# Perceiver block on one core: first norm of the prologue split between VectorE and ScalarE, root table and value weights moved in ScalarE's load list

## Chip, core and metric

The kernel runs on one core of a Trainium2 chip. The metric is device time in microseconds of one execution; the median of three runs is compared. Engines are called as the profile calls them: PE (TensorE), DVE (VectorE), ACT (ScalarE), POOL (GpSimd) and SP (SyncE). ACTq and SPq are the instruction queues of ScalarE and SyncE, from which loads are issued.

## What is computed

Two sequences of 512 tokens with 512 features pass through three stages, each added to its input:

```python
x = x + xattn(layernorm(x), ctx, mask, Wq, Wk, Wv, Wo)   # 16 heads; 8192 context rows of 384
x = x + attn(layernorm(x), ...)                          # causal, amplitude and phase, 16 heads
x = x + moe(layernorm(x), ...)                           # 16 experts, two per token, capacity 64
layernorm: (x - mean) / sqrt(var + 1e-5)                 # over the 512 features
```

All is float32. The mask of the cross-attention is given as bytes; masked keys get a large negative bias. Only the first layernorm, ahead of the cross-attention, is touched by the change (a helper that a later stage calls too is rewritten for both).

## The kernel before

Tokens lie in eight tiles of 128 (four for each sequence, `TB` = 4). The cross-attention runs over 16 chunks of 1024 context rows (eight for each sequence) and, within each, over four groups of four heads; all of its matmuls are on TensorE, in four column or row strips at a time (`columns`, L216). It takes most of the span.

Ahead of that loop stands a prologue, `prepare` (L290 to L402). From L569 on, instructions keep the written order on each engine, so what a line comes behind in the text is what it comes behind on its queue. The prologue does the following:

- Loads. SyncE issues four token tiles of sequence 0 (L294), the mask and the context of chunk 0 in six loads of 256 KB (L256, L260), the tokens of sequence 1 (L304, 1 MB), the mask and context of chunk 1 (three loads of 512 KB) and Wo (L306). ScalarE issues the mask as a table (L296), four slices of Wq (L299), three of Wk and three of Wv (L302).
- The first key that isn't masked is found for each sequence (L309 to L345), and its context column is gathered by six indirect loads of POOL (L354), three for each sequence, with an index from VectorE for each (L353).
- The norm of sequence 0: `pieces[0]` to `pieces[3]` are the statistics of a tile (`stats`, L101), with the search for the first key between them; `pieces[4]` is `scale` (L106), which takes the root of all four variances on ScalarE (L82), its reciprocal and one Newton step on VectorE (L83 to L87); `pieces[5]` to `pieces[8]` scale a tile on VectorE (`normed`, L110 to L121).
- Each tile is turned by four TensorE transposes into PSUM (L193) and copied out by ScalarE (L194). When all four are turned, `query(0, 0)` projects the queries of the first head group (32 matmuls, L373), and `first_keys(0)` projects the gathered key (L376 to L389).

After that come the keys of the first step (L420), the maxima of the scores, and a list of further work beside them (`beside`, L589): the norm of sequence 1, the other queries, the values (which read Wv for the first time) and `first_keys(1)`.

`scale_of`, `scaled` and `normed` are also offered to a later stage (L895 to L911), which calls them with a tile to keep (`keep`): three tiles' root, scaling on ScalarE, then the fourth.

```python
def scaled(i):
    if i == 0:
        nc.vector.scalar_tensor_tensor(less[:, :TB-1], mv[:, :TB-1, 0], -1.0, rstd[:, :TB-1], ...)
    tiles.append(keep[:, i, :])
    nc.scalar.activation(tiles[-1], xs[...], AF.Identity, bias=less[:, i:i+1], scale=rstd[:, i:i+1])
```

Of the kernel before, what the change touches and what calls it, by code (L numbers as in the profile page):

```python
# [11 lines left out]
F32 = mybir.dt.float32  # L12
# [3 lines left out]
AF = mybir.ActivationFunctionType  # L16
# [4 lines left out]
P = 128  # L21
B, S, D = 2, 512, 512
H, HD = 16, 32
NT = B * S // P
TB = S // P
ND = D // P
M, CD = 8192, 384
NC = CD // P
# [14 lines left out]
def perceiver_kernel(ctx: ExitStack, tc: tile.TileContext, a, out: bass.AP):  # L43
    nc = tc.nc
# [26 lines left out]
    def m4(name, shape=(P, 2, S)):  # L71
        return mid.tile(list(shape), F32, tag="m4", name=name)
# [5 lines left out]
    def inv_sqrt(pool, y, v, tag):  # L78

        shape = list(v.shape)  # L80
        t = pool.tile(shape, F32, tag=f"{tag}_t", name=f"{tag}_t")
        nc.scalar.activation(t, v, AF.Sqrt)  # L82
        nc.vector.reciprocal(y, t)  # L83
        nc.vector.tensor_tensor(t, y, y, ALU.mult)
        nc.vector.tensor_tensor(t, t, v, ALU.mult)
        nc.vector.tensor_scalar(t, t, -0.5, 1.5, ALU.mult, ALU.add)
        nc.vector.tensor_tensor(y, y, t, ALU.mult)  # L87

    lnp = ctx.enter_context(tc.tile_pool(name="ln", bufs=2))
    eps = const.tile([P, 1], F32, name="eps")  # L90
    nc.gpsimd.memset(eps, LN_EPS)

    def norm_pieces(b, keep=None, aside=False):


        pool = lnp
        mv = pool.tile([P, TB, 2], F32, tag="ln_mv", name="ln_mv")
        v = pool.tile([P, TB], F32, tag="ln_v", name="ln_v")
        rstd = pool.tile([P, TB], F32, tag="ln_r", name="ln_r")

        def stats(i):  # L101
            st = pool.tile([P, 6], F32, tag="ln_st", name="ln_st")
            nc.vector.bn_stats(st, xs[:, b * TB + i, :])
            nc.vector.bn_aggr(mv[:, i, :], st)

        def scale():  # L106
            nc.vector.tensor_scalar_add(v, mv[:, :, 1], LN_EPS)
            inv_sqrt(pool, rstd, v, "ln")

        def normed(i):  # L110
            if keep is not None:
                xn = keep[:, i, :]
            elif i % 2 == 0:
                tiles.pair = m4("ln_xn", (P, 2, D))
                xn = tiles.pair[:, 0, :]
            else:
                xn = tiles.pair[:, 1, :]
            nc.vector.tensor_scalar(
                xn, xs[:, b * TB + i, :], mv[:, i, 0:1], rstd[:, i : i + 1], ALU.subtract, ALU.mult
            )  # L120
            tiles.append(xn)  # L121

        less = pool.tile([P, TB], F32, tag="ln_less", name="ln_less")
        t = pool.tile([P, TB], F32, tag="ln_t2", name="ln_t2")

        def newton():
            nc.vector.reciprocal(rstd, t)
            for out, x, y in ((t, rstd, rstd), (t, t, v)):
                nc.gpsimd.tensor_tensor(out, x, y, ALU.mult)
            nc.gpsimd.tensor_scalar(t, t, -0.5, 1.5, ALU.mult, ALU.add)  # L130
            nc.gpsimd.tensor_tensor(rstd, rstd, t, ALU.mult)
            nc.gpsimd.tensor_tensor(less, mv[:, :, 0], rstd, ALU.mult)
            nc.gpsimd.tensor_scalar(less, less, -1.0, None, ALU.mult)

        def normed_aside(i):
            if i % 2 == 0:
                tiles.pair = m4("ln_xn", (P, 2, D))
            tiles.append(tiles.pair[:, i % 2, :])
            nc.scalar.activation(
                tiles[-1], xs[:, b * TB + i, :], AF.Identity, bias=less[:, i : i + 1], scale=rstd[:, i : i + 1]  # L140
            )

        class Tiles(list):
            pass

        tiles = Tiles()

        def scale_of(lo, hi):

            some = slice(lo, hi)  # L150
            nc.scalar.activation(t[:, some], mv[:, some, 1], AF.Sqrt, bias=eps)
            nc.vector.tensor_scalar_add(v[:, some], mv[:, some, 1], LN_EPS)
            nc.vector.reciprocal(rstd[:, some], t[:, some])
            nc.vector.tensor_tensor(t[:, some], rstd[:, some], v[:, some], ALU.mult)
            nc.vector.tensor_tensor(t[:, some], t[:, some], rstd[:, some], ALU.mult)
            nc.vector.tensor_scalar(t[:, some], t[:, some], -0.5, 1.5, ALU.mult, ALU.add)
            nc.vector.tensor_tensor(rstd[:, some], rstd[:, some], t[:, some], ALU.mult)

        def scaled(i):

            if i == 0:
                nc.vector.scalar_tensor_tensor(
                    less[:, : TB - 1], mv[:, : TB - 1, 0], -1.0, rstd[:, : TB - 1], ALU.mult, ALU.mult
                )
            tiles.append(keep[:, i, :])
            nc.scalar.activation(
                tiles[-1], xs[:, b * TB + i, :], AF.Identity, bias=less[:, i : i + 1], scale=rstd[:, i : i + 1]
            )

        tiles.stats, tiles.scale_of, tiles.scaled, tiles.normed = stats, scale_of, scaled, normed  # L170
        pieces = [lambda i=i: stats(i) for i in range(TB)]
        if aside:
            pieces += [
                lambda: nc.gpsimd.tensor_scalar(v, mv[:, :, 1], LN_EPS, None, ALU.add),
                lambda: nc.scalar.activation(t, v, AF.Sqrt),
                newton,
            ]
        else:
            pieces += [scale]
        pieces += [lambda i=i: (normed_aside if aside else normed)(i) for i in range(TB)]  # L180
        return tiles, pieces
# [48 lines left out]
    def cross_attention(tail):  # L230

        with ExitStack() as st:
# [17 lines left out]
            def load_chunk(i, pieces=1):  # L250
                b, c = chunks[i]
                t = [m4("ctx", (P, CH)) for j in range(NC)]
                src = a["ctxT"][b].rearrange("(c p) k -> p c k", p=P)
                m8 = sm.tile([P, CH], U8, tag="m8", name="m8")
                row = a["mask_BxS2_bf1"][b : b + 1, c * CH : (c + 1) * CH]
                nc.sync.dma_start(m8, row.to_broadcast([P, CH]))  # L256
                for hf in range(pieces):
                    at = slice(hf * CH // pieces, (hf + 1) * CH // pieces)
                    for j in range(NC):
                        nc.sync.dma_start(t[j][:, at], src[:, j, c * CH + at.start : c * CH + at.stop])  # L260
                ctx_tiles[i], mask_tiles[i] = t, m8

            wkv = [m4("wkv", (P, 2, D)) for _ in range(NC)]
            wk, wv = ([wkv[j // 2][:, j % 2, :] for j in range(n, n + NC)] for n in (0, NC))
# [25 lines left out]
            def prepare(qp):  # L290
# [6 lines left out]
                wq = b8("wq")  # L297
                for c in range(ND):
                    nc.scalar.dma_start(wq[:, c, :], a["L0_xattn_Wq"][c * P : (c + 1) * P, :])  # L299
                for w, n in ((wk, "Wk"), (wv, "Wv")):  # L300
                    for j in range(NC):
                        nc.scalar.dma_start(w[j], a[f"L0_xattn_{n}"][j * P : (j + 1) * P, :])  # L302
                load_chunk(0, 2)
                nc.sync.dma_start(xs[:, TB:, :], x_in[:, TB:, :])  # L304
                load_chunk(1)
# [18 lines left out]
                tiles, pieces = norm_pieces(0)  # L324
# [22 lines left out]
                cf1 = [qp.tile([P, 1], F32, name=f"cf_{i}") for i in range(NC * B)]  # L347
                cf = qp.tile([P, NC, B], F32, name="cf")
                table = a["ctxT"].rearrange("b c (k o) -> (b c k) o", o=1)
                for b in range(B):  # L350
                    for c in range(NC):
                        i = c * B + b
                        nc.vector.tensor_scalar(at_i[i], at[:, b : b + 1], float((b * CD + c * P) * M), None, ALU.add)  # L353
                        nc.gpsimd.indirect_dma_start(  # L354
                            out=cf1[i],
                            out_offset=None,
                            in_=table,
                            in_offset=bass.IndirectOffsetOnAxis(ap=at_i[i], axis=0),
                        )
                anyb = qp.tile([P, B], F32, name="anyb")  # L360
                nc.vector.tensor_scalar_min(anyb, pf[:, :B], 1.0)
                nc.vector.tensor_scalar(kmul, anyb, is_bias, BIG, ALU.mult, ALU.mult)
# [4 lines left out]
                def turned(b, tiles, i):  # L367
                    turn(Bank(bank()), "j", tiles[i], xnT[b][:, :, i * P : (i + 1) * P], nc.scalar.copy)
# [19 lines left out]
                            )  # L388
                    nc.vector.tensor_copy(kf[:, :, b], pk[:, :NG])  # L389

                for f in pieces[3:5]:
                    f()
                for i in range(TB):
                    pieces[5 + i]()
                    turned(0, tiles, i)
                query(0, 0)
                first_keys(0)
                tiles, pieces = norm_pieces(1)
# [170 lines left out]
            ctx.enter_context(tc.manual_schedule())  # L569
            with tc.tile_pool(name="xa_q", bufs=1) as qp:  # L570
                norm, more = prepare(qp)

                def keys_of(n, hf):
# [48 lines left out]
            for n, (i, g) in enumerate(steps):  # L622
                b, c = chunks[i]
                pieces = [(k_half, n + 2, hf) for hf in range(2)] if n + 2 < len(steps) else [None] * 2
# [11 lines left out]
                for kt in range(NKT):  # L636
# [17 lines left out]
                    else:  # L654
                        part = None
                        if pieces[kt // 2]:
                            f, k, x = pieces[kt // 2]
# [924 lines left out]
```

## Time and profile before

| what | value |
| --- | --- |
| median of three runs | 2997.42 us (2994.43 to 2998.41) |
| time of the profiled execution | 2998.28 us |
| its span, first to last instruction | 2996.6 us |
| mean granted clock of TensorE | 0.987 |
| TensorE busy from 0 to 30 us | 16.35 us |
| TensorE busy from 60 to 2350 us | 2285.87 us |
| mean DMA share and rate from 0 to 30 us | 0.89, 308 GB/s |

The profile lists for each engine what ran, from when and for how long, and for idle time the event that ended it. The chain of work is followed back from the last instruction to what released it. A wait is put down to the releaser that came last. Durations of DMA issues are those of the issuing instruction; from the first of a group to the end of its last, waits between are counted in.

### The profile page before, as it was taken

What the parts mean: (1) busy time and instruction counts of PE and PEld (TensorE: products, weight loads), DVE (VectorE), ACT (ScalarE), POOL (GpSimd) and SP (SyncE); (2) the same over time, 40 slices, a digit from 0 to 9 for tenths busy, and PEclk for the clock granted to TensorE, in tenths of its full rate; (3) what the DMA queues carried; (4) which work ended last, traced back from release to release, by engine and by line L of the source; (5) the groups of instructions that cost most, each with busy time, mean ns of one, the idle gap of its engine ahead of it and who ended that gap; (6) DMA issues with size and microseconds to landing.
All of it is one profiled execution on the core that took longest, in us unless ns stands there. A gap on an engine that the chain in (4) does not pass through costs nothing.

```text
span 2996.6 us, 65645 instructions
## 1 busy us (share of the span) xinstructions
PE 2912.9 (97%) x28459; PEld 1128.1 (38%) x28459; DVE 1960.1 (65%) x3292; ACT 1397.1 (47%) x2614; POOL 2177.5 (73%) x880
## 2 busy tenths in 40 slices
PE   7999999999999999999999999999999999999985
PEld 2333333333333333333333333333333332345574
DVE  5567776677777677766777777777767666556422
ACT  1345555555555555544555555555555436563311
POOL 1598888888888888978888888888888872012022
PEclk9999999999999999999999999999999999999988
DMA  3000000000000000000000000000000002001374
GB/s 124 1 24 2 24 2 24 1 24 2 24 3 23 5 21 9 17 1 24 2 24 1 24 1 24 1 24 1 24 2 1 29 29 72 1 29 62 103 249 138
DMA packets 48145, 89.73 MB, mean 30 GB/s; under 512 B 4720, under 2 KB 23152, under 8 KB 47856
## 3 DMA queue, kind: packets, MB, share of 16 engines
q1 hardware_dynamic: 40832, 70.31, 7.0%
q0 software_dynamic: 2752, 8.39, 0.9%
q10 hardware_dynamic: 4272, 6.83, 0.7%
q8 instruction: 223, 3.65, 0.5%
q14 instruction: 66, 0.54, 0.1%
HBM read 77.13 MB, written 8.39 MB: 29 GB/s over the span
## 4 chain that ended last, share of the span: by engine, by line
PE 93%; DVE 3%; ACT 1%; DMA 1%; issue 1%; POOL 0%; ACTq 0%; POOLq 0%; DVEq 0%
PE s L220 31%; PE s L449 18%; PE s L514 16%; PE s L462 15%; PE s L481 4%; PE s L1244 2%; PE ph L953 2%; PE s L541 2%; PE po L970 1%; DVE cm L471 1%; PE s L1338 1%; PE s L1379 1%; DVE acc L549 1%; DMA r<-results,get 0%; DVE acc L529 0%
## 5 line engine op out<-in xcount | busy, mean ns | idle before, releaser
L680 POOL TENSOR_TENSOR es<-es,e 128x2048 f32<-128x2048 f32 x374 | 1700.7, 4547 | 54.9 <-ACT e L483 38.1
L483 ACT ACTIVATE e<-s 128x512 f32<-128x512 f32 x2048 | 1057.4, 603 | 1111.0 <-PE s L481 1111.0
L471 DVE TENSOR_REDUCE cm<-s 128x1 f32<-128x512 f32 x2048 | 1271.0, 683 | 332.3 <-PE s L449 332.2
L449 PE MATMUL s<-k,qT 32*128 32x512 f32 x4096 | 588.1, 641 | 3.4 <-DVE cm L471 1.9
L462 PE MATMUL s<-qT,k 32*128 32x512 f32 x4096 | 554.8, 593 | 3.1 <-ACT e L483 2.3
L514 PE MATMUL s<-e,v 128*32 128x512 f32 x4096 | 495.3, 600 | 1.1 <-DVE cm L471 1.0
L680 POOL TENSOR_TENSOR es<-e 128x2048 f32<-128x2048 f32 x63 | 286.1, 4541 | 242.9 <-ACT e L483 242.9
L220 PE MATMUL s<-wkv,ctx 128*32 128x512 f32 x3072 | 365.4, 596 | 0.4
L220 PE MATMUL s<-ctx,wkv 128*32 128x512 f32 x3072 | 356.5, 597 | 0.5
L462 PEld LDWEIGHTS s<-qT,k 32*128 32x128 f32 x4096 | 282.3, 184 | 185.1 <-issue 106.3
L529 DVE TENSOR_TENSOR acc<-acc,s 128x512 f32<-128x512 f32 (+1 forms) x359 | 207.8, 604 | 138.6 <-PE s L514 138.1
L449 PEld LDWEIGHTS s<-k,qT 32*128 32x128 f32 x4096 | 161.8, 183 | 330.7 <-issue 259.0
L514 PEld LDWEIGHTS s<-e,v 128*32 128x32 f32 x4096 | 107.4, 109 | 320.0 <-DVE cm L471 160.9
L481 PE MATMUL s<-rows,mb 4*128 4x512 bf16 x2048 | 218.0, 376 | 0.0
L425 DVE SCALAR_TENSOR_TENSOR k<-s,kf,m 128x512 f32<-128x512 f32 x128 | 96.1, 751 | 171.7 <-PE s L220 171.7
L220 PEld LDWEIGHTS s<-ctx,wkv 128*32 128x32 f32 x3072 | 87.2, 109 | 236.5 <-issue 155.5
L220 PEld LDWEIGHTS s<-wkv,ctx 128*32 128x32 f32 x3072 | 86.9, 109 | 214.3 <-issue 125.9
L440 ACT COPY v<-s 128x512 f32<-128x512 f32 x128 | 74.9, 585 | 98.7 <-PE s L220 77.8
L537 DVE TENSOR_TENSOR acc<-acc,s 128x1024 f32<-128x1024 f32 x56 | 68.4, 1221 | 71.1 <-ACT s L536 71.1
L1325 POOL TENSOR_SCALAR_AFFINE_SELECT e<-e 128x512 f32<-128x512 f32 x32 | 22.3, 708 | 120.0 <-ACT e L1323 120.0
L481 PEld LDWEIGHTS <-mb 4*128 4x128 bf16 x2048 | 68.5, 93 | 105.5 <-issue 97.4
L1293 POOL TENSOR_TENSOR rest<-scm,parts 128x16 f32<-128x16 f32 x8 | 2.0, 253 | 124.3 <-DVE parts L1291 121.2
(277 smaller groups left out, 1917.0 us busy)
## 6 DMA issues: line engine op xcount, KB each, us to landing
ctx<-in_ctxT_dram SPq DMA_DIRECT2D x45, 512.0 KB
wg<-in_L_ffn_w_gate_dram SPq DMA_DIRECT2D x16, 512.0 KB
wf<-in_L_ffn_w_fc_dram SPq DMA_DIRECT2D x16, 512.0 KB
wp<-in_L_ffn_w_proj_dram SPq DMA_DIRECT2D x16, 512.0 KB
results<-res ACTq DMA_DIRECT2D x32, 128.0 KB
m<-in_mask_BxS_bf_dram SPq DMA_DIRECT2D x16, 128.0 KB
w_wq_phiT<-in_wq_phiT_dram SPq DMA_DIRECT2D x2, 1024.0 KB
w_wq_ampT<-in_wq_ampT_dram SPq DMA_DIRECT2D x2, 1024.0 KB
```

Source lines behind the costliest of these rows:

```text
L220: nc.tensor.matmul(out[q], lhsT[:, q], rhs, start=start, stop=stop)
L425: nc.vector.scalar_tensor_tensor(k[:, keys], bank, kf[:, g, b : b + 1], mask_tiles[i][:, keys], ALU.subtract, ALU.mult)
L440: nc.scalar.copy(v[:, kt % (NKT // 2), :], bank)
L449: nc.tensor.matmul(s, qT(chunks[i][0], g, r, slice(qt * P, (qt + 1) * P)), k_tiles[n][r, hf * S : (hf + 1) * S], start=True, stop=True,)
L462: nc.tensor.matmul(s, k_tiles[n][r, keys], qT(chunks[i][0], g, r, slice(0, S)), start=True, stop=False)
L471: nc.vector.tensor_reduce(cms[g][chunks[i][1] % 2][:, qt, j : j + 1, hf], ss[j], AX.X, ALU.max)
L481: nc.tensor.matmul(ss[j], bias_tiles[i][r4, keys], rows[r4, :], start=False, stop=True)
L483: nc.scalar.activation(e[:, j, :], ss[j], AF.Exp)
L514: nc.tensor.matmul(av[j * HD : (j + 1) * HD, :], v_tiles[i][kt // (NKT // 2)][:, kt % (NKT // 2), h * HD : (h + 1) * HD], e[:, j, :], star ...
L529: nc.vector.tensor_tensor(dst, dst, src, ALU.add)
L537: nc.vector.tensor_tensor(acc[g], acc[g], pa.unsqueeze(1).to_broadcast([P, 2, S]), ALU.mult)
L680: nc.gpsimd.tensor_tensor(es, first if kt == 1 else es, e, ALU.add)
```

## The change

Four things are changed. The load list of ScalarE gets a root of a constant (so the root's table is loaded there) between Wq and Wk, and loses Wv. The gathers are split by sequence. The norm of sequence 0 is done as in the later stage: the root of three tiles, tile 0 scaled by VectorE, tiles 1 and 2 by ScalarE, then statistics, root and scaling of tile 3. The loads of Wv are issued by ScalarE after the root of tile 3, ahead of the copies of the turned tiles; then come the gathers of sequence 1. `scaled` no longer needs `keep` and forms the shift `less` at its first call.

```diff
         def scaled(i):
-            if i == 0:
+            if not tiles.less:
+                tiles.less = True
                 nc.vector.scalar_tensor_tensor(
                     less[:, : TB - 1], mv[:, : TB - 1, 0], -1.0, rstd[:, : TB - 1], ALU.mult, ALU.mult
                 )
-            tiles.append(keep[:, i, :])
+            if keep is not None:
+                tiles.append(keep[:, i, :])
+            else:
+                if i % 2 == 0:
+                    tiles.pair = m4("ln_xn", (P, 2, D))
+                tiles.append(tiles.pair[:, i % 2, :])
...
+        tiles.less = False
...
-                for w, n in ((wk, "Wk"), (wv, "Wv")):
-                    for j in range(NC):
-                        nc.scalar.dma_start(w[j], a[f"L0_xattn_{n}"][j * P : (j + 1) * P, :])
+                nc.scalar.activation(qp.tile([P, 1], F32, name="warm"), eps, AF.Sqrt)
+                for j in range(NC):
+                    nc.scalar.dma_start(wk[j], a["L0_xattn_Wk"][j * P : (j + 1) * P, :])
...
-                for b in range(B):
+                def gather(b):
                     for c in range(NC):
...
+                gather(0)
+                tiles.scale_of(0, TB - 1)
+                tiles.normed(0)
+                for i in range(1, TB - 1):
+                    tiles.scaled(i)
+                pieces[TB - 1]()
+                tiles.scale_of(TB - 1, TB)
+                tiles.normed(TB - 1)
+                for j in range(NC):
+                    nc.scalar.dma_start(wv[j], a["L0_xattn_Wv"][j * P : (j + 1) * P, :])
+                gather(1)
...
-                for f in pieces[3:5]:
-                    f()
                 for i in range(TB):
-                    pieces[5 + i]()
                     turned(0, tiles, i)
```

## Prediction

> **What bounds the kernel now.** I read the page's chain first, to see who sets the end, then the chain cut to the first 60 us, because the diff touches only the prologue, and then ScalarE's queue, the waits of SyncE's queue and TensorE's rows there. The page:
>
> ```profile
> PE 2912.9 (97%) x28459; PEld 1128.1 (38%) x28459; DVE 1960.1 (65%) x3292; ACT 1397.1 (47%) x2614; POOL 2177.5 (73%) x880
> ...
> PE 93%; DVE 3%; ACT 1%; DMA 1%; issue 1%; POOL 0%; ACTq 0%; POOLq 0%; DVEq 0%
> ```
>
> TensorE is the path for 93% of the span. Between 60 and 2350 us it is busy 2285.87 of 2290 us, so a shift of the prologue passes to the end almost one for one, and nothing else in the diff can move the rest. The chain in order of time, early part (start, us, what):
>
> ```profile
> 0.79 2.91 DMA mc<-in_mask_BxS_bf_dram
> ...
> 3.72 6.41 DMA wq<-in_L_xattn_Wq_dram
> ...
> 10.15 0.34 ACTq L302
> ...
> 10.52 1.28 ACT L82
> ...
> 11.81 0.21 ACT ln_t L82
> ...
> 13.93 3.69 PE s L193 x16
> ...
> 17.64 0.59 ACT xnT L194
> ...
> 18.28 10.18 PE s L220 x138
> ```
>
> The root (L82) comes last on ScalarE's queue, behind ten weight loads. Each load waits until an earlier one has landed: the fourth Wq (3.72) for the mask (landed 3.70), the last Wv (10.15) for that Wq (landed 10.13). The trace names eight landing semaphores, given in turn to the loads of ScalarE's and SyncE's queues together, so a load waits for the one eight before it, of either queue. SyncE's waits say the same:
>
> ```profile
> SPq L304 <- DMA wkv<-in_L_xattn_Wv_dram: 1.2, 1, 1.2
> ...
> SPq L260 <- DMA wkv<-in_L_xattn_Wk_dram: 0.7, 2, 0.3
> ```
>
> ScalarE alone, in order of time (start, us, what, idle before):
>
> ```profile
> 4.96 2.23 ACTq L302 DMA_DIRECT2D wkv<-in_L_xattn_Wk_dram  x3
> 7.22 3.26 ACTq L302 DMA_DIRECT2D wkv<-in_L_xattn_Wv_dram  x3
> 10.52 1.28 ACT L82 ACT_TABLE_LOAD   x1 [10.52 <-DMA wkv<-in_L_xattn_Wk_dram]
> ```
>
> What matters is when TensorE can start the first query matmul (18.28): after the last of four copies of transposed tokens (L194).
>
> **The change, part by part.**
>
> *Root earlier.* The table (1.28 us) and a warm-up root (0.21) move to 4.06, the end of the Wq issues: done at 5.6. The three Wk loads took 2.23 us, waits included; from 5.6 they end at 7.9, or 8.5 if the third must wait for the third Wq (its successor on that semaphore went out at 8.12). VectorE's statistics of the third tile end at 7.75, its three gather indices and the variance sum by 8.8 (rows of 8.30 to 8.67 and 0.17 us). So the first root is done by 8.8. From the reciprocal to the first scaled tile was 12.05 to 13.11 = 1.06 us, then 0.82 to the first transpose. First transpose at 10.7, 3.2 us before 13.93. The Trainium skill ("ScalarE: Activation LUTs", section What ACT_TABLE_LOAD costs) counts about 2.66 us for a table switch, with a drain; here the root follows the load in 0.01 us, so I take 1.28. With 2.66 the Wk loads would end near 9.2 and the first transpose be 0.5 later, still ahead of what follows.
>
> *Scaling split.* Removed: one VectorE root chain over four tiles and three of its four scalings (0.55 each). Added: a second chain for one column (five small rows, 0.17 to 0.23 each), one row for the shift (0.23), two ScalarE scalings (nearest row: the 0.59 copy). In order: tile 0 on VectorE 9.9 to 10.45; shift to 10.65; tiles 1 and 2 on ScalarE to 12.0; the second root to 12.2; its chain 1.06, tile 3 scaled by 13.85; its four transposes from 14.1 at 0.21 each (15 gaps of 3.69 us) to 14.95. Statistics of tile 3 (0.87) hide under ScalarE's scalings; without that cover they would cost 0.87. If nothing else intervened, copies would follow tile by tile and the query start at 15.8: 2.5 us gained.
>
> *Wv behind the second root.* This is where it is decided: three loads stand on ScalarE's queue at 12.2, and the four copies behind them. By itself an issue takes 0.42 us, 1.3 for three, done by 13.5, before tile 3 is even transposed. But ScalarE must wait for the semaphores. The DMA page of the skill ("DMA: Bandwidth & Descriptors", section Issuing engines are not separate DMA queues) calls the sequencer's time to start a DMA usually small beside the DMA; that would give the 15.8. The row gives 3.26 for these three, so 15.5 if they wait as before. And they now rank behind loads of context and tokens that SyncE can issue sooner: the lag from a load's issue to that of the eighth after it was 6.4 us (3.72 to 10.15) and 6.6 (8.12 to 14.73, L304). If Wv follows loads issued from 8 to 10 us, it goes out from 14.5 to 16.5. Ends: 13.5 (no wait) and 21 or more (below). I take 16.3, nearest to the 6.5 us lag. Copies in a row took 2.05 us for four (71.79, second batch): query at 18.4, 0.1 later than before. The DMA engines are full (0.96 to 1.06) until 27 us, so no total transfer time is saved; context lands earlier, but in the before trace TensorE didn't wait for it.
>
> *TensorE's clock.* Now transposes end at 14.95 and TensorE stands till 18.4, 3.4 us. In the trace the query matmuls begin slow straight after transposes:
>
> ```profile
> 18.28 4.16 PE L220 MATMUL s<-xnT,wq 128*32 128x512 f32 x32 [0.68 <-ACT xnT L194]
> ...
> 29.46 3.64 PE L220 MATMUL s<-xnT,wq 128*32 128x512 f32 x32
> ```
>
> 4.16 against 3.64 us; the first eight last up to 1063 ns against a median of 592, and the first group of four takes 0.855 us where a warm one takes 0.43. So an entirely slow query is 6.84 us, a loss of 3.2, where before lost 0.52. The skill ("TensorE: Matmul & The Clock Gate", Part 1) says half rate until about 3.4 us of sustained work, in a free-running window, and again after as long an idle one. Here the query was slow for only 1.1 us, having 3.7 us of transposes before it; by that row alone I would add 0. By the rule, with the stand between, 3.4 to 4.2 us of it are slow: four to five groups at 0.43, 1.8, less 0.5 already paid. A row that has a stand like this one: after 36.9 TensorE idled 2.15 us and the granted clock from 39.9 to 43.3 was 0.50. It speaks for the rule; I take +1.3, ends -0.5 and +2.9. That same window cost 1.6 us (2.09 against 1.14 and 3.39 against 2.78) and may fall elsewhere: +/-1.6, not counted.
>
> *At nothing:* the second batch of gathers goes on POOL after tile 3 (about 14.2 to 18, 1.25 each), and the bias (1.19, from 16.27) behind it, to about 19; nobody reads either before 38. The first keys' copies on VectorE (15.22 to 17.23) wait for the first gathers, which don't move, and TensorE needs them only after the query. Wv is first read at 46.4. SyncE stood for 136.7 us afterwards, so its delay costs nothing. Without that cover the bias would cost 1.2 us and the gathers up to 3.7.
>
> *Sum:* query start +0.1, clock +1.3: +1.4 us on the profiled execution (span 2996.6, time 2998.28, which is 0.9 above the median). On the median 2997.42: 2998.8.
>
> **Rivals.**
>
> A, the forecast: ScalarE held by Wv to about 16.3, TensorE slow afterwards, +1.4, 2998.8. Chance 0.50.
>
> B, Wv hardly waits (ScalarE free by 13.5 to 14): query at 15.8, transposes straight before it, clock as before: -2.5, 2994.9. For it: the issue rows (0.42). Against: every load after the eighth waited. 0.28.
>
> C, slower: the third Wv takes the semaphore of a 512 KB context load or of Wo. Transfers run on to about 27.6 us (213 GB/s from 27 to 28), so ScalarE could be held to between 21 and 27, and the copies with it: query at 23 to 29, +5 to +11, and +1.3 for the clock: +6 to +12, 3003.7 to 3009. It passes the bound of 0.2% from a release at about 21. Against: Wv stands only some three loads behind SyncE's, and eight back from there is a 256 KB one. 0.07.
>
> D, the change doesn't do what it says: the third Wk is ranked behind context loads and waits for the fourth Wq (10.13), so the root is again at 10.5. Then transposes from 12.4 to 16.6, Wv out by 16.5, query at 18.6, a short stand: +0.3 and +0.5, 2998.2. 0.15.
>
> **Numbers.** 0.2% is 6 us, about what a measurement of this kernel can tell from no change. Only C passes it upwards (0.05 with what of C stays below); downwards B with a lucky clock window is -4.6, so 0.02 is left for what I don't see. Range: from B with the clock's 1.6 to A with its upper ends (+2.9 for the clock, +2 for the release): 2993.5 to 3003.0.
>
> **What would show it.** Root near 8.5 and first transposes near 10.7 (else D); ScalarE's Wv issues spanning 12.2 to about 16.3 (B: to 13.5; C: past 21), four copies behind them; the first query matmul near 18.4, with more than eight matmuls near 1 us. The prediction is wrong if the query starts by 16 or after 21, or if the slices after 60 us differ by more than a microsecond.

## Result and profile after

The changed kernel takes 3003.68 us (median of 17 runs, 3000.63 to 3005.81) against 2997.42 of the kernel before (17 runs): ratio 1.0020, 95% interval 1.0013 to 1.0026. That is 6.3 us slower (3.9 to 7.8), outside the range of the prediction, and on the side of rival C. The profiled execution has a span of 3002.0 us, 5.4 more than before; the other 0.9 of the 6.3 us is that the profiled execution of the kernel before lies above its median.

The page of the changed kernel, busy time by engine and the chain's shares, shows nothing: the path is TensorE's as before.

```profile
PE 2914.4 (97%) x28459; PEld 1126.5 (38%) x28459; DVE 1959.5 (65%) x3297; ACT 1399.5 (47%) x2618; POOL 2178.9 (73%) x880
...
PE 93%; DVE 3%; DMA 1%; ACT 1%; issue 1%; POOL 0%; ACTq 0%; SPq 0%; POOLq 0%; DVEq 0%
```

The chain in order of time, cut to the first 60 us, shows it at once (start, us, what):

```profile
11.51 8.05 DMA xs<-in_x_dram
...
19.58 0.33 ACTq L379
...
19.96 2.06 ACT xnT L201 x4
...
22.07 11.29 PE s L227 x139
```

A transfer of tokens that nobody needs yet (the second sequence, first read at 36.84 us) is on the path: the issue of the third Wv load (L379) waits for it to land, the four copies wait for that issue, and the first query waits for the copies. ScalarE's own order of time:

```profile
8.16 0.30 ACT L151 ACTIVATE ln_t<-ln_mv,eps 128x3 f32<-128x3 f32 x1 [2.47 <-DVE first L349]
10.59 1.52 ACT L172 ACTIVATE ln_xn<-xs,ln_less,ln_r 128x512 f32<-128x512 f32 x2 [2.13 <-DVE ln_less L163]
12.02 0.28 ACT L151 ACTIVATE ln_t<-ln_mv,eps 128x1 f32<-128x1 f32 x1
15.92 4.00 ACTq L379 DMA_DIRECT2D wkv<-in_L_xattn_Wv_dram  x3
19.96 2.05 ACT L201 COPY xnT<-s 128x512 f32<-128x512 f32 x4 [7.66 <-DMA xs<-in_x_dram]
```

The bracket on the last line is what to look for: ScalarE computed nothing for 7.66 us, and what ended that was a landing, not an engine. TensorE meanwhile:

```profile
10.54 2.89 PE L200 MATMUL s<-ident,ln_xn 128*128 128x128 f32 x12 [2.95 <-DVE ln_xn L118]
13.90 1.11 PE L200 MATMUL s<-ident,ln_xn 128*128 128x128 f32 x4 [0.48 <-DVE at L362]
22.07 5.27 PE L227 MATMUL s<-xnT,wq 128*32 128x512 f32 x32 [7.04 <-ACT xnT L201]
```

Transposes begin 3.4 us earlier than before, and the query 3.79 later, after a stand of 7.04 us (a stand is a stretch in which TensorE has nothing to run).

| | predicted | measured | before |
| --- | --- | --- | --- |
| first root done | 8.8 | 8.46 | 12.02 |
| first transpose | 10.7 | 10.54 | 13.93 |
| tile 3 scaled | 13.85 | 13.85 | 15.30 |
| last transpose over | 14.95 | 15.01 | 17.61 |
| third Wv issued | 16.3 | 19.91 | 10.49 |
| query starts | 18.4 | 22.07 | 18.28 |
| query lasts | 5.5 | 5.27 | 4.16 |
| first exponential of the attention | +1.4 | 107.94 (+4.97) | 102.97 |

The last row is read from these two lines, the kernel before and the changed one:

```profile
102.97 1.57 ACT L483 ACTIVATE e<-s 128x512 f32<-128x512 f32 x3 [2.29 <-PE s L481]
...
107.94 2.06 ACT L501 ACTIVATE e<-s 128x512 f32<-128x512 f32 x4 [2.29 <-PE s L499]
```

The sum is 22.07 - 18.28 = 3.79 for the start and 5.27 - 4.16 = 1.11 for the query, 4.90 of the 4.97 us by which the first exponential is late. From there the lag hardly moves: 4.94 us near 400, 4.56 near 2430. It then goes to 5.80 (near 2620), because TensorE's granted clock is 0.50 for 6.83 us around 2520 and was for 3.41 before; late in the kernel it moves again (3.4 near 2900), and it is 5.4 at the end. That step is not of the change alone: e1 and e8 below, which were ahead of the kernel before, have the double stretch too.

### The profile page after: what moved, and what is told of

Read it like the earlier page. It is cut to its first block, busy times and chain, and to the rows that moved or that the text cites. A ratio compares the mean times of both kernels' runs of the same rounds, so it can differ in the third digit from the quotient of the medians.

```text
span 3002.0 us, 65654 instructions
## 1 busy us (share of the span) xinstructions
PE 2914.4 (97%) x28459; PEld 1126.5 (38%) x28459; DVE 1959.5 (65%) x3297; ACT 1399.5 (47%) x2618; POOL 2178.9 (73%) x880
## 3 DMA queue, kind: packets, MB, share of 16 engines
q10 hardware_dynamic: 4272, 6.83, 0.7%
## 4 chain that ended last, share of the span: by engine, by line
PE 93%; DVE 3%; DMA 1%; ACT 1%; issue 1%; POOL 0%; ACTq 0%; SPq 0%; POOLq 0%; DVEq 0%
PE s L227 31%; PE s L467 17%; PE s L532 16%; PE s L480 15%; PE s L499 4%; PE s L1262 2%; PE ph L971 2%; PE s L559 2%; PE po L988 1%; DVE cm L489 1%; PE s L1356 1%; PE s L1397 1%; DVE acc L567 1%; DVE acc L547 0%; POOL r L1016 0%
```

## Experiments

Each is compared with runs of the kernel before on the same chip; the chips differ (2998.66, 2987.19 and 2998.2 us for the kernel before in the three sessions). The ratio is given as recorded and can differ by 0.0004 from the quotient of the medians. "Lag" is the start of the first exponential less 102.97; it compares one profiled execution with that of the kernel before, whatever the chip.

**e1: Wv behind the copies.**

```diff
-                for j in range(NC):
-                    nc.scalar.dma_start(wv[j], a["L0_xattn_Wv"][j * P : (j + 1) * P, :])
                 gather(1)
...
                 for i in range(TB):
                     turned(0, tiles, i)
+                for j in range(NC):
+                    nc.scalar.dma_start(wv[j], a["L0_xattn_Wv"][j * P : (j + 1) * P, :])
```

> The changed kernel with one edit: the three Wv loads stand behind the four copies of turned tiles on ScalarE's queue, not ahead of them. Theory 1 (ScalarE is held at the third Wv until the 1 MB token load lands, with the copies behind it, and TensorE is slow after the stand): the copies follow the transposes, query starts near 15.8 us, not 22.07, the hold at Wv to about 19.6 stays but nobody waits; query 4.2 to 5.3 us long; span near 2995.5, the time 1.5 to 3 us under before. Theory 2 (the split norm itself costs, by its second root chain and by early transposes): last transpose and query later than 15.8 or slower, span 3000 or more. Theory 3 (Wv or context comes too late from memory): query early, but TensorE gaps before 50 us, span near 3002.

Measured: 2995.27 us, ratio 0.9992 (0.9983 to 1.0000, so the interval reaches no change), span 2995.5, lag -1.75. TensorE in order of time:

```profile
15.31 5.29 PE L227 MATMUL s<-xnT,wq 128*32 128x512 f32 x32 [0.68 <-ACT xnT L201]
```

and ScalarE:

```profile
14.67 0.58 ACT L201 COPY xnT<-s 128x512 f32<-128x512 f32 x1 [1.00 <-issue]
16.50 4.45 ACTq L413 DMA_DIRECT2D wkv<-in_L_xattn_Wv_dram  x3
20.99 0.60 ACT L393 ACTIVATE qT<-s 128x512 f32<-128x512 f32 x1 [5.73 <-PE s L227]
```

A wait of the same kind, 4.45 us over the three issues (4.00 in the changed kernel), stands on the same queue, now with the query's scaling behind it, which is not needed until the keys are done. Moving three issues past four copies is worth 6.72 us of the lag. Theory 2 (the split norm delays the query) and 3 (late data) fall; TensorE has no new gap. The query itself is slow, at the upper end of what was expected.

**e2: the token load last.** Only the order of SyncE's loads is changed, so that another load is the eighth before the third Wv.

```diff
-                nc.sync.dma_start(xs[:, TB:, :], x_in[:, TB:, :])
                 load_chunk(1)
                 nc.sync.dma_start(wo, a["L0_xattn_Wo"].rearrange("(c p) d -> p c d", p=P))
+                nc.sync.dma_start(xs[:, TB:, :], x_in[:, TB:, :])
```

> The changed kernel with one edit: SyncE's 1 MB load of the second sequence's tokens goes behind Wo, so that the load eight before the third Wv is the sixth context load and not the token load. Theory 1: ScalarE's hold ends when that context load has landed, near 17 us instead of 19.58; four copies, query near 19.3; span about 2999.3, time 1.5 to 2.5 us over before. Theories 2 and 3: query stays at about 22, span 3002.

Measured: 3000.31 us, ratio 1.0008 (1.0000 to 1.0017), span 2998.0, lag +1.90. ScalarE:

```profile
14.85 1.86 ACTq L379 DMA_DIRECT2D wkv<-in_L_xattn_Wv_dram  x3
16.75 2.05 ACT L201 COPY xnT<-s 128x512 f32<-128x512 f32 x4 [4.53 <-DMA ctx<-in_ctxT_dram]
```

The releaser is now a context load, and the hold ends at 16.71 instead of 19.91. So which load happens to be eight before sets the length of the hold; only the order of SyncE's later loads was changed. Query at 18.86 (expected 19.3).

**e3: Wv early again**, with the rest of the change kept.

```diff
                 for j in range(NC):
                     nc.scalar.dma_start(wk[j], a["L0_xattn_Wk"][j * P : (j + 1) * P, :])
+                for j in range(NC):
+                    nc.scalar.dma_start(wv[j], a["L0_xattn_Wv"][j * P : (j + 1) * P, :])
...
                 tiles.normed(TB - 1)
-                for j in range(NC):
-                    nc.scalar.dma_start(wv[j], a["L0_xattn_Wv"][j * P : (j + 1) * P, :])
```

> The changed kernel with the Wv loads back right behind Wk, ahead of the first root; everything else of the change stays (table among the loads, split norm, split gathers). Theory 1: the third Wv waits for the fourth Wq (landing near 10), the first root runs at about 10.5, first transpose near 12.5, last near 16.7, no hold after it: query near 17.5, 0.8 us before 18.28, span 2995 to 2997. Theory 2: the split costs, query after 18.5, span over 2998.

Measured: 2997.07 us, ratio 0.9999 (0.9990 to 1.0007), lag +1.33. The root came at 10.95 and the query at 18.04 (expected 17.5), 0.24 before the kernel before, but it took 5.61 us, so nothing is gained:

```profile
18.04 5.61 PE L227 MATMUL s<-xnT,wq 128*32 128x512 f32 x32 [0.68 <-ACT xnT L201]
```

Against e1 it shows what "Wv later" is worth when it holds nobody: 15.31 against 18.04, 2.7 us.

**e4: the kernel before, only Wv late** (behind the single root, ahead of the copies).

```diff
-                for w, n in ((wk, "Wk"), (wv, "Wv")):
-                    for j in range(NC):
-                        nc.scalar.dma_start(w[j], a[f"L0_xattn_{n}"][j * P : (j + 1) * P, :])
+                for j in range(NC):
+                    nc.scalar.dma_start(wk[j], a["L0_xattn_Wk"][j * P : (j + 1) * P, :])
...
                 for f in pieces[3:5]:
                     f()
+                for j in range(NC):
+                    nc.scalar.dma_start(wv[j], a["L0_xattn_Wv"][j * P : (j + 1) * P, :])
                 for i in range(TB):
```

> The kernel before with one part of the change: the Wv loads behind the (single) root, ahead of the copies; norm, table and gathers as before. The load eight before the third Wv is here the sixth context load. Theory 1: root near 10.4, transposes from 12.5, but ScalarE held to about 17, copies to 19.2, query near 19.2, slower first matmuls: span 2998 to 2999. Theory 2: without the split nothing is lost: query at 18.3 or earlier, span 2996.6 or less.

Measured: 3000.68 us, ratio 1.0007 (1.0001 to 1.0014). The profile has the hold without any split of the norm:

```profile
15.08 2.27 ACTq L393 DMA_DIRECT2D wkv<-in_L_xattn_Wv_dram  x3
17.39 2.05 ACT L194 COPY xnT<-s 128x512 f32<-128x512 f32 x4 [6.47 <-issue]
```

The bracket names no releaser here, but the copies again follow the third Wv issue. TensorE:

```profile
19.50 5.34 PE L220 MATMUL s<-xnT,wq 128*32 128x512 f32 x32 [3.26 <-ACT xnT L194]
```

Query at 19.50 and 5.34 us long (expected 19.2). The lag is +0.81 only: it was +2.4 at the first score maximum and lost 1.6 again near 43 us, where TensorE's clock was slow before and isn't here. Its profiled span, 2994.6, is 2.0 under that of the kernel before while its median is slower; the profiled execution (2996.34 us) is the fastest of its 21, part of the difference is the clock late in the kernel, and one execution doesn't settle it. The interval and the query's start speak for theory 1, the span alone doesn't.

**e8: Wv on SyncE's queue**, at the same place in the text, with the same loads eight before.

```diff
-                    nc.scalar.dma_start(wv[j], a["L0_xattn_Wv"][j * P : (j + 1) * P, :])
+                    nc.sync.dma_start(wv[j], a["L0_xattn_Wv"][j * P : (j + 1) * P, :])
```

> The changed kernel with the three Wv loads issued by SyncE, at the same place in the text, with the same loads eight before them (the third again waits for the 1 MB token load). Theory 1 (what costs is that ScalarE's copies stand behind the wait): SyncE stands until about 19.6, nobody behind it is needed, query near 15.3 and about 5.3 us long as in e1, 1.75 us ahead of the kernel before from 100 us on. Rival (the loads, their order or their late landing cost by themselves): query late or TensorE gaps, 3 us or more behind.

Measured: 2994.30 us, ratio 0.9990 (0.9982 to 0.9999), lag -1.60, query at 15.30. The waits of SyncE's queue (us in total, times, longest):

```profile
SPq L379 <- DMA xs<-in_x_dram: 2.3, 1, 2.3
```

and TensorE:

```profile
15.30 5.43 PE L227 MATMUL s<-xnT,wq 128*32 128x512 f32 x32 [0.67 <-ACT xnT L201]
```

The wait for the token load is there, at the same time (SyncE's three issues span 16.51 to 20.42), and costs nothing. So the loads themselves, their order and their landing cost nothing here; what costs is what stands behind the wait.

**e5 and e7: TensorE's stand filled**, to measure the clock's term: matmuls on loaded weights between the last transpose and the first query of the changed kernel. e7 has `range(5)` in place of `range(10)`.

```diff
                     pq = bank()
+                    if b == 0 and g == 0:
+                        for i in range(10):
+                            columns(pq, wq[:, 0, :P], wq[:, 1, :], True, True)
```

> The changed kernel with one addition: 40 matmuls of 128x512 (ten groups of four, on two loaded slices of Wq, into the bank that the first query overwrites) between the last transpose and the first query, so that TensorE doesn't stand during ScalarE's hold. The hold stays. Theory 1 with the clock as its second term: query starts at 22.07 as in the changed kernel, but takes about 3.64 us, not 5.27; from 100 us on 1.5 us ahead of the changed kernel, still 3.4 behind the kernel before. Rival (the slow query is not due to the stand, but to its own operands or to transfers going on): query again about 5.3 us, no gain.

Measured: 2993.62 us against 2987.19 (ratio 1.0018, 1.0012 to 1.0025), lag +7.77. I had sized it wrongly: the 40 float32 matmuls are 80 rows of the trace (so the query's 32 rows are 16 matmuls), and the filling took 10.59 us and itself held the query to 24.99. TensorE:

```profile
14.57 10.59 PE L227 MATMUL s<-wq 128*32 128x512 f32 x80
24.99 3.61 PE L227 MATMUL s<-xnT,wq 128*32 128x512 f32 x32
```

> As e5, with half the filling: it took 10.59 us there (each float32 matmul is two rows of the trace), so 5.3 us here, over before the copies are. The hold stays as in the changed kernel. Theory 1: query starts when the fourth copy is done (22.0), takes 3.6 us instead of 5.27; from 100 us on 3.3 us behind the kernel before (changed kernel: 4.97), or 1.6 more or less with the clock window near 45 us. Rival: query about 5.3 us, 4.97 behind.

Measured: 3002.48 us, ratio 1.0017 (1.0009 to 1.0025), lag +5.63. The lag was expected at +3.3. The copies were over only at 22.70 (the hold ended at 20.62), 3.1 us after the filling:

```profile
14.55 5.09 PE L227 MATMUL s<-wq 128*32 128x512 f32 x40
22.76 5.25 PE L227 MATMUL s<-xnT,wq 128*32 128x512 f32 x32 [3.11 <-ACT xnT L201]
```

In the stretch in which this query begins, TensorE's granted clock is 0.50 (from and to, length, busy time of PE, PEld, DVE, ACT and POOL with rows, clock, DMA share, GB/s):

```profile
22.64:26.05 3.41, 3.29 (x16) 0.80 (x20) 0.00 (x0) 0.07 (x1) 0.00 (x0) 0.50 1.04 396
```

As a saving, both miss. Taken together they answer the question: the same 32 rows with the same operands, transfers going on in both, take 3.61 us straight behind other matmuls and 5.25 after a stand of 3.11. So a stand of this length is enough to make the query 1.6 us slower, and operands and transfers are not the cause. It is not needed for that: in e1, e3 and e8 the query is as slow behind a stand of under 0.7 us.

**e6: e1 with TensorE kept at work** ahead of the transposes, in time in which it had nothing to do.

```diff
                 nc.tensor.matmul(pf[:, :B], ones[:B, :], dg, start=True, stop=True)
+                for i in range(12):
+                    nc.tensor.matmul(pm[:, :P], ident, ident, start=True, stop=True)
```

> The kernel with Wv behind the copies (e1), with twelve 128x128 matmuls of the identity added on TensorE in its idle time ahead of the first transpose (7.6 to 10.2 us). Theory 1: TensorE's clock is granted before the query; query starts near 15.3 as in e1 or up to 0.2 earlier and takes 3.6 to 4.2 us instead of 5.29, so from 100 us on it is 3 us ahead of the kernel before (e1: 1.75); time about 2994. Rival (the clock follows from something other than TensorE's own work just before): query again 5.3 us, as e1.

Measured: 2984.60 us against 2987.19 on that chip, ratio 0.9990 (0.9983 to 0.9996), lag -5.36. TensorE:

```profile
7.51 4.48 PE L348 MATMUL s<-ident 128*128 128x128 f32 x24
...
14.98 3.64 PE L227 MATMUL s<-xnT,wq 128*32 128x512 f32 x32 [0.67 <-ACT xnT L201]
```

The added matmuls ended at 11.99, 1.8 us later than foreseen, and delayed the first transpose to 11.83, yet the query is earlier than in e1, because the transposes behind them run at twice the pace (12 in 1.47 us, 2.89 in the changed kernel). Of the lag, -3.30 is the query's start and -0.52 its length; the other 1.56 is a slow stretch of TensorE (39.9 to 43.3 before), which does not occur here. On the same chip the medians differ by 2.6 us only (the interval of the ratio is 1.2 to 5.1 us), less than the lag. Its interval and that of e8 overlap, on different chips; which of the two is faster isn't shown, but both intervals lie below the kernel before.

## Why the prediction was wrong

- *What bounds, and that a prologue shift passes through:* right. The lag is 4.97 at the first exponential and between 4.56 and 4.97 up to 2430 us. That the slices after 60 us would differ by less than a microsecond was off: the clock near 2520 us added 1.2.
- *Root earlier, scaling split:* right to 0.4 us in the first four rows of the table. D (the root held by Wk) did not come: all three Wk were issued by 7.92.
- *Wv behind the second root:* this is the step that failed. The mechanism was named (ScalarE waits for the load eight before, with the copies behind it); its size was taken from a lag of 6.5 us between a load and the eighth after it, on loads of 256 KB, and from "some three loads behind SyncE's". In fact all of SyncE's prologue loads had taken their turns on the semaphores first: Wv are the 26th to 28th load, and eight before them are the fifth and sixth context load and the tokens of the second sequence. That one is 1 MB, was issued at 11.51, where the prediction took loads issued from 8 to 10, and landed 8.05 us later, where it took 6.5; the later issue and the longer landing make about 1.5 us each. The term of the sum, a release at 16.3 with a reach of 2 us, measured 19.91. The query's start, 22.07, is past the 21 that the prediction had named as a sign of being wrong. e2 shows the size hanging on that load (16.71 with another in its place), e8 and e1 that the wait matters only for what is queued behind it.
- *Clock:* +1.3 was predicted and +1.11 measured. The size is right, the reason only in part, so the agreement is partly luck. e7 shows that a stand of 3.11 us makes the query slow; but e1, e3 and e8, whose stand is as short as in the kernel before (0.68 us), pay as much (5.29, 5.61 and 5.43 us). In the changed kernel the weight loads of the query's groups of four show where the slow part ends:

```profile
24.63 0.20 PEld L227 LDWEIGHTS s<-xnT,wq 128*32 128x32 f32 x4 [0.66 <-issue]
25.45 0.12 PEld L227 LDWEIGHTS s<-xnT,wq 128*32 128x32 f32 x4 [0.62 <-issue]
25.88 0.12 PEld L227 LDWEIGHTS s<-xnT,wq 128*32 128x32 f32 x4 [0.31 <-issue]
```

  Up to there a group takes about 0.85 us, afterwards 0.43; the trace's clock record has the grant at 25.40, 3.3 us after the query's start. So of the two grounds for the term, the rule of the Trainium skill ("TensorE: Matmul & The Clock Gate", Part 1), half rate for about 3.4 us, came nearer (3.3 here) than the row alone, which gave 0.
- *Rivals:* B was excluded in this kernel but is what e1 and e8 do, at 15.3 (predicted 15.8). Without the clock it would be -2.97; with the query at 5.29 us the lag is -1.75, so taking the clock at nothing in B was wrong too. C had the right course and the wrong load: not a 512 KB load or Wo, but the token load, the very one that stood in the trace of before as waiting for Wv (L304). Its release is 1 us short of the point of 21 at which C was to pass 0.2%; the profiled execution is 0.18% slower, the median 0.21%. A chance of 0.07 was too little for a term whose upper end I had left open.
- *Where the gain went:* the 3.4 us at the first transpose are real. 2.6 of them are left at the end of the transposes (15.01 against 17.61). These go into TensorE's stand, and 3.8 us more; then come 1.1 for the slow query.
- *Range:* its ends, 2993.5 and 3003.0, are not quite the sums of the terms that were named for them, 2993.3 and 3002.4; the measured time lies above both.

## What to carry to other kernels

A load issued from a compute engine's queue can be a wait on that queue. Here it lasted until the load had landed whose semaphore it took over, whatever that load was for (19.58 us for the third Wv behind the token load); before moving such an issue, count which load that is and list what is queued behind. An issue that is not urgent belongs behind the urgent work of its engine (e1) or on a queue with nothing behind it (e8). An earlier start gains only if the whole stretch up to the bounding engine moves with it; a gap that is opened in TensorE's work can be paid a second time in its clock (1.6 us in e7).

## What was not expected of the hardware

- Loads are issued while ScalarE loads a table. In the changed kernel the table runs from 4.19 to 5.47 us, and the first two Wk issues stand beside it:

```profile
4.19 1.28 ACT L308 ACT_TABLE_LOAD   x1 [4.19 <-DMA mc<-in_mask_BxS_bf_dram]
5.10 0.82 ACTq L310 DMA_DIRECT2D wkv<-in_L_xattn_Wk_dram  x2
```

  The first Wk went out at 5.10 us, 0.14 later than before (4.96) and not 1.28; in both traces it waits for the first Wq, whose semaphore was full at 5.08 (4.94 before).
- What TensorE's clock goes by is not read out of these traces. The changes in each clock record lie 3.41 us or a multiple of it apart. In the 3.41 us ahead of the first grant TensorE was busy for 2.73 us in the kernel before and for 2.86 in e4, in the latter with transposes alone; a stretch with 2.29 us (e1) or 2.26 (e3) ahead of the query brought no grant. But no limit on the busy time fits all stretches: none was granted after 2.79 us in the changed kernel (11.75 to 15.16) and 2.95 in e5 (11.43 to 14.85). The clock was withdrawn after 0.42 (e7), 1.25 (before) and 2.30 us (e3, 39.13 to 42.55), but not after 1.87 (e6, 31.24 to 34.66) or 2.00 (e4, 37.27 to 40.69). So why the query is slow in e1, e3 and e8, though TensorE stood for only 0.68 us before it, stays open. That the second root of the split norm interrupts the transposes by 0.5 us is one candidate; no run takes it alone. What is shown is that work on TensorE ahead of the transposes removes it (e6: 3.64 us).
